# Layer 0's folded sums: four products of 128x32 for two steps, ahead of the weighted values

## The chip, the core and the metric

One core of a Trainium2 chip runs the whole program. The time is device microseconds (us) of one execution; three executions of the kernel before took 980.66, 981.69 and 983.73 us. The core's engines are TensorE (PE in the profile; its weight loads are shown apart as PEld), VectorE (DVE), ScalarE (ACT), GpSimd (POOL) and SyncE (SP). Each engine runs its own instructions in the order of the program and waits on semaphores for the others. SP does nothing here but issue DMAs, which stand in one queue.

## The reference

Two cross attentions follow one another. Both read the same context of 128 keys per batch row; the queries are 2 x 2048 positions of width 512.

```
attn = einsum('bqhd,bkhd->hbqk', qh, kh)          # layer 0: 16 heads of 64
attn = attn * mask
attn = attn - max(attn)                           # one maximum over everything
attn = exp(attn) * mask
attn = attn / (sum(attn, over keys) + 1e-15)
out  = einsum('hbqk,bkhd->bqhd', attn, vh) @ Wo + bo
x    = layernorm(out + residual) * gamma + beta   # and then layer 1 in the same manner
```

What matters here is layer 0's denominator, `sum(attn, over keys)`: for each head and each query one sum over the 128 keys, which lie on the 128 partitions. A sum over partitions is a product with a matrix of ones on TensorE.

## The kernel before, in words

The 4096 queries are eight blocks `t` of 512, the 16 heads four groups `g` of four. A *step* is one pair `(t, g)`. Layer 0 goes through the 32 steps two at a time: `order` (L386) lists them, and the loop at L512 runs 16 iterations `i`, of which iteration `i` makes the scores of steps `2i` and `2i+1` and finishes the two steps of iteration `i-1`. All five engines are scheduled by hand: the order in which the Python code emits instructions is the order on each engine and on SP's queue.

For one iteration after the first the order is:

- `queries_pair` (L336): seven products that make the queries of both steps. Inside it, `exponentials0` (L424) is called for both steps of iteration `i-1`: a maximum on DVE (L430), the exponential on ACT (L434), the mask on POOL (L435). The results are the tiles `sm`, keys on partitions, four heads of 512 queries each.
- `sums_of_folded(i-2)` (L464), if that iteration is in `FOLDED` (L384).
- `scores0` of the first step (L388): four products `st` of 64 rows (L396), two instructions on DVE that apply the mask and take maxima (L409), and two DMAs on SP: a store of the 128x2 maxima, `top` (L418), and a load, `every` (L421), that broadcasts them to all partitions and so waits until the store has landed.
- For iteration `i-1`, if it is in `FOLDED`: `shift` and `fold` of its first step. Then `attend0` of its first step (L477): two sets of four products `psu` (L491) with copies by ACT (L495) and a 512 KB store `u` on SP (L496).
- `shift` of the second step, `scores0` of the second step with its `top` and `every`, `attend0` of the other step of `i-1`, and `fold` of it.

**Folding.** `shift` (L451) has ACT copy one half of the keys of a step's `sm` onto the other 64 partitions, and `fold` (L458) has DVE add the other half. After that 64 partitions hold what has to be summed for one step, and the two steps of an iteration lie in the two halves of one tile `fold` of 128 partitions. `sums_of_folded` then runs, for each of four heads, one product of 64x32 per step, into two PSUM tiles, and `store_sums` (L439) copies each of them to a tile `den` and stores four of its rows on SP (L442).

**Not folded.** `FOLDED` holds eleven iterations: 0, 1, 3, 4, 5, 7, 8, 9, 11, 12 and 13. For the steps of the others, `attend0` makes the sums itself, directly ahead of its `psu`: four products of 128x32 with ones (L484), an ACT copy to a tile `den` and a store. So in the loop's iterations 3, 7, 11 and 15 there are both kinds: the folded sums of `i-2`, and the direct sums of both steps of `i-1` (in the last one, one of these two comes after the loop).

**Tiles that are shared.** The PSUM pool `p_av` (L81) has two buffers, which `sums_of_folded`, `attend0` and two of the seven products take in turn. The pool `a2` has two buffers for each of its tiles, and so there are two of the SBUF tile `den` (L440): the copy that fills one has to wait until the stores that read its previous contents have landed. The tile `fold` has one buffer (pool `w1`, L454).

The line that sets the place of the folded sums is L539 to L545:

```
queries_pair(p, g, order[2 * i - 2 : 2 * i])
if i - 2 in FOLDED:
    sums_of_folded(i - 2)
...
scores0(*steps0[0])
```

After the loop come the last two steps, layer 0's output projection (`pso`, L671) and layer 1. The denominators are read back from DRAM in two halves (L197).

Of the kernel before, what the change touches and what calls it, by code (L numbers as in the profile page):

```python
# [9 lines left out]
F32 = mybir.dt.float32  # L10
# [6 lines left out]
P = 128  # L17
TB = 512
# [6 lines left out]
def two_cross_attentions(  # L25
# [28 lines left out]
    nc = tc.nc  # L54
# [14 lines left out]
    def where(t):  # L69
        return t // SPB, (t % SPB) * TB  # L70
# [5 lines left out]
    const = ctx.enter_context(tc.tile_pool(name="const", bufs=1))  # L76
# [12 lines left out]
    def av_tile(name):  # L89
        return p_av.tile([P, TB], F32, tag="av", name=name)  # L90
# [4 lines left out]
    nc.vector.memset(mhalf, -0.5)  # L95
    ones = const.tile([P, 32], F32, tag="ones", name="ones")
    nc.vector.memset(ones, 1.0)


    idle = mm_tile("idle")  # L100
# [7 lines left out]
    for g in range(NG):  # L108
        for r in range(4):
            rows = slice(32 * r, 32 * (r + 1))  # L110
# [13 lines left out]
    def chunks(w):  # L124
        return w.rearrange("(c p) m -> p c m", p=P)
# [6 lines left out]
    def row(pool, v, name, tag=None):  # L132
# [17 lines left out]
    den_dram = [  # L150
        dram.tile([len(h) * H, TB], F32, tag=f"den_{n}", name=f"den_{n}") for n, h in enumerate(halves)
    ]
# [4 lines left out]
    def den_rows(of, t, g):  # L157
        r0 = (t % (NB // 2)) * H + 4 * g
        return of[t // (NB // 2)][r0 : r0 + 4, :]
# [46 lines left out]
    with tc.tile_pool(name="w1", bufs=1) as w1, tc.tile_pool(name="a2", bufs=2) as a2, tc.tile_pool(  # L206
        name="a3", bufs=3
# [12 lines left out]
        def load_x(t):  # L220

            b, q0 = where(t)
            pool, tag = (big, "big") if t // 2 % 2 else (xs, "xt")
            tiles = []
            for h in range(2):
                xt = pool.tile([P, 2, TB], F32, tag=tag, name=f"xt_{t}_{h}")
                nc.sync.dma_start(xt, xT[b, q0 // TB, h])
                tiles.append(xt)
            xts[t] = tiles

        def load_mask(t):
            b, q0 = where(t)
            m = a4.tile([P, TB], F32, tag="mask", name=f"mask_{t}")
            nc.gpsimd.dma_start(m, maskT[b, :, q0 : q0 + TB])
            return m
# [22 lines left out]
        def keys0(e):  # L258
            ps = mm_tile(f"psk0_{e}")
            for c in range(ND):  # L260
                nc.tensor.matmul(
                    ps[:, : B * K], wk0s[:, e // 2, c, (e % 2) * P : (e % 2 + 1) * P], cTs[:, c, :],
                    start=(c == 0), stop=(c == ND - 1),
                )
            nc.scalar.activation(
                k0[:, e, :], ps[:, : B * K], AF.Identity, bias=bk0s[:, e : e + 1]
            )

        def values0(b, n):
            ps = mm_tile(f"psv0_{b}_{n}")  # L270
            at = slice(n * TB, (n + 1) * TB)
            for c in range(ND):
                nc.tensor.matmul(
                    ps, cTs[:, c, b * K : (b + 1) * K], wv0s[c][:, at],
                    start=(c == 0), stop=(c == ND - 1),
                )
            nc.vector.tensor_tensor(v0[:, b, at], ps, bv0s[n], ALU.add)
# [106 lines left out]
        FOLDED = [n for n in range(NB // 2 * NG - 2) if n % NG != NG - 2]  # L384
        last4 = w1.tile([P, 4], F32, tag="last4", name="last4")
        order = [(2 * p + n, g) for p in range(NB // 2) for g in range(NG) for n in range(2)]  # L386
# [49 lines left out]
                    s, s, masks[t].unsqueeze(1).to_broadcast([P, 2, TB]), ALU.mult  # L436
                )

        def store_sums(t, g, ps, copy=nc.scalar.copy):  # L439
            den = a2.tile([P, TB], F32, tag="den", name=f"dens0_{t}_{g}")  # L440
            copy(den, ps)  # L441
            nc.sync.dma_start(  # L442
                den_rows(den_dram, t, g), den.rearrange("(j n) q -> j n q", n=32)[:, 0, :]
            )

        folded = {}

        def half_keys(n):
            return slice(n * P // 2, (n + 1) * P // 2)

        def shift(i, n):  # L451

            if n == 0:
                folded[i] = w1.tile([P, 4, TB], F32, tag="fold", name=f"fold_{i}")  # L454
            p = pairs0[order[2 * i + n]].rearrange("p n j q -> p (n j) q")
            nc.scalar.copy(folded[i][half_keys(n)], p[half_keys(1 - n)])  # L456

# [5 lines left out]

        def sums_of_folded(i):  # L464
            f = folded.pop(i)
            ps = [av_tile(f"den0_{i}_{n}") for n in range(2)]
            for j in range(4):
                for n in range(2):
                    rows = slice(n * P // 2, (n + 1) * P // 2)
                    nc.tensor.matmul(  # L470
                        ps[n][32 * j : 32 * (j + 1), :], ones[rows, :], f[rows, j, :],
                        start=True, stop=True,
                    )
            for n in range(2):
                store_sums(*order[2 * i + n], ps[n], (nc.vector.tensor_copy, nc.scalar.copy)[n])

        def attend0(t, g):  # L477

            b, _ = where(t)
            p = [probs0[t, 2 * g + j // 2][:, j % 2, :] for j in range(4)]  # L480
            if order.index((t, g)) // 2 not in FOLDED:
                ps = av_tile(f"den0_{t}_{g}")
                for j in range(4):
                    nc.tensor.matmul(ps[32 * j : 32 * (j + 1), :], ones, p[j], start=True, stop=True)  # L484
                store_sums(t, g, ps)
            u = a3.tile([P, 2, TB], F32, tag="u", name=f"u0_{t}_{g}")
            for half in range(2):
                ps = av_tile(f"psu0_{t}_{g}_{half}")
                for j in range(4):
                    d = (4 * g + j) * DK + half * 32  # L490
                    nc.tensor.matmul(  # L491
                        ps[32 * j : 32 * (j + 1), :], v0[:, b, d : d + 32], p[j],
                        start=True, stop=True,
                    )
                nc.scalar.copy(u[:, half, :], ps)  # L495
            nc.sync.dma_start(u_dram[t, g], u.rearrange("p j q -> p (j q)"))  # L496
# [15 lines left out]
        for i in range(len(order) // 2):  # L512
            p, g = i // NG, i % NG
            steps0 = order[2 * i : 2 * i + 2]
            if g == (2 if p == 0 else 1) and p + 1 < NB // 2:
                for t in (2 * p + 2, 2 * p + 3):
                    load_x(t)
                    masks[t] = load_mask(t)
            if p == 0:
                for e in (2 * g, 2 * g + 1):  # L520
                    keys0(e)
            if i == 1:
                for n in range(E // TB):
                    values0(1, n)
            if i == 4:
                w = w1.tile([P, 2 * ND, TB], F32, tag="first", name="wkv1")
                wk1s, wv1s = w[:, :ND, :], w[:, ND:, :]
                nc.sync.dma_start(wk1s, chunks(wk1))
                nc.sync.dma_start(wv1s, chunks(wv1))
            if i == 12:  # L530
                sums0(0, w1, "sums0", 1)
            if i == 13:
                load_wo0()

            if i == 0:
                queries0(0, 0)
                queries0(0, 1)
            else:
                queries_pair(p, g, order[2 * i - 2 : 2 * i])  # L539
                if i - 2 in FOLDED:  # L540
                    sums_of_folded(i - 2)
            if i == len(order) // 2 - 1:
                for n in range(NG):
                    fetch_u(0, n)
            scores0(*steps0[0])  # L545
            if i == 0:
                queries0(1, 0)
                queries0(1, 1)
                weight_sums(1)
            else:  # L550
                if i - 1 in FOLDED:
                    shift(i - 1, 0)
                    fold(i - 1, 0)
                attend0(*order[2 * i - 2])
                if i - 1 in FOLDED:
                    shift(i - 1, 1)
            if i == 0:
                token_sums_1(0)
            elif g == NG - 1 and p + 1 < NB // 2:
                token_sums_1(p + 1)  # L560
            scores0(*steps0[1])
            if i == 0:
                for n in range(E // TB):
                    values0(0, n)
                token_sums_2(0)
                weight_sums(2)
            elif i < len(order) // 2 - 1:
                attend0(*order[2 * i - 1])
                if i - 1 in FOLDED:
                    fold(i - 1, 1)  # L570
            if g == NG - 1 and p + 1 < NB // 2:
                token_sums_2(p + 1)
            if i in (1, 2):
                weight_sums((3, 0)[i - 1])
# [38 lines left out]
        ps = av_tile("whole")  # L613
        nc.tensor.matmul(ps[:, :4], one_row, diag, start=True, stop=True)
        for n in range(2):
            t, g = order[n - 2]
# [532 lines left out]
    t = NB - 1  # L1149
    for i in range(NQ):  # L1150
        project1(t, i, 0)
    for i in range(NQ):
# [5 lines left out]
        else:  # L1158
            ps = open1[t, i]
# [68 lines left out]
```

## Time and profile before

| | |
|---|---|
| time, three executions | 980.66, 981.69, 983.73 us, median 981.69 |
| span of the profiled execution | 977.3 us |
| its own time | not given apart; 4.4 us lie between its span and the median |
| PE busy | 958.0 us, 98% of the span |
| DVE, POOL, ACT busy | 731.8, 483.3, 414.9 us |
| granted TensorE clock, mean | 0.997 |
| folded sums on PE (L470) | 176 instructions in eleven groups, 12.0 us |
| direct sums on PE in the same layer (L484) | 80 instructions in ten groups, 10.7 us |
| DVE copies of sums (L441) | 11 of 692 ns |
| ACT copies of sums (L441) | 21 of 575 ns |
| SP stores of sums (L442) | 32 of 8 KB |

Each f32 product appears as two PE instructions, so sixteen L470 are eight products. A row of the timeline gives the start, how long the merged instructions took, engine, line, output and inputs, and in square brackets how long the engine was idle before and what released it. The ends of matmuls are modelled, so that PE looks busy even where it waits a little; the distance between the starts of two groups is what can be trusted. Of a DMA, SP's row shows the issue alone; when it lands is told by the trace's record of semaphore updates.

### The profile page before, as it was taken

How to read it: one execution, taken by the hardware profiler on the slowest of the kernel's cores; microseconds unless marked ns; L12 is line 12 of the kernel's file. 1: busy time of each engine (PE TensorE's matmuls, PEld its weight loads, DVE VectorE, ACT ScalarE, POOL GpSimd, SP SyncE). 2: the span in 40 equal slices, each digit the busy share in tenths (PEclk: the TensorE clock that was granted, in tenths of full speed). 3: DMA queues.
4: the chain of work that ended last, by engine and by line, in shares of the span. 5: the costliest groups of instructions: out<-in, count | busy, mean ns of one | idle time of the engine just before them, and what ended most of it. 6: DMA issues, size and time to landing. Idle time of an engine off the chain costs nothing.

```text
span 977.3 us, 12755 instructions
## 1 busy us (share of the span) xinstructions
PE 958.0 (98%) x4628; PEld 448.4 (46%) x4628; DVE 731.8 (75%) x1093; ACT 414.9 (42%) x637; POOL 483.3 (49%) x403
## 2 busy tenths in 40 slices
PE   8999999999999999999999999999999999999996
PEld 4444333333333334474544644645545545545442
DVE  2577777878878872249469869879789689698867
ACT  1145345545534644044534434434344444344351
POOL 1044454543453546685453934925835736546153
PEclk9999999999999999999999999999999999999998
DMA  9314265225223436534632542632723724403311
GB/s 337 126 49 141 55 175 155 56 57 182 60 79 86 120 104 201 181 128 157 243 128 87 188 160 87 238 110 89 263 82 119 251 90 155 167 1 151 111 44 43
DMA packets 51325, 128.46 MB, mean 131 GB/s; under 512 B 9440, under 2 KB 13280, under 8 KB 47680
## 3 DMA queue, kind: packets, MB, share of 16 engines
q1 hardware_dynamic: 49536, 125.03, 38.5%
q0 software_dynamic: 1152, 2.10, 0.9%
q8 instruction: 36, 0.59, 0.3%
q10 hardware_dynamic: 576, 0.53, 0.2%
q14 instruction: 25, 0.20, 0.1%
HBM read 101.46 MB, written 26.18 MB: 131 GB/s over the span
## 4 chain that ended last, share of the span: by engine, by line
PE 76%; DVE 4%; POOL 2%; issue 1%; ACT 0%; POOLq 0%; DVEq 0%; ACTq 0%
PE pso L671 22%; PE ps L347 12%; PE pso L1026 10%; PE psq L822 8%; PE psu L491 5%; PE st L396 4%; PE s L948 3%; PE mx L873 3%; PE u L996 3%; PE psq L860 1%; PE tr L727 1%; PE den L470 1%; PE den L484 1%; DVE sums L903 1%; PE psk L591 1%
## 5 line engine op out<-in xcount | busy, mean ns | idle before, releaser
L435 POOL TENSOR_TENSOR sm<-sm,mask 128x1024 f32<-128x1024 f32 x64 | 150.4, 2372 | 202.4 <-ACT sm L434 191.4
L671 PE MATMUL pso<-wo,uT 128*128 128x512 f32 x512 | 229.2, 599 | 0.2 <-POOL uT L182 0.2
L671 PEld LDWEIGHTS pso<-wo,uT 128*128 128x128 f32 x512 | 94.5, 190 | 117.2 <-issue 109.1
L658 POOL TENSOR_TENSOR rstd<-rstd,mhalf 128x1 f32<-128x1 f32 x64 | 35.2, 550 | 213.8 <-DVE shift L662 213.7
L434 ACT ACTIVATE sm<-sm,ncs 128x1024 f32<-128x1024 f32 x64 | 70.0, 1141 | 107.6 <-DVE ncs L431 107.5
L1026 PE MATMUL pso<-wq,ctx 128*128 128x512 f32 x256 | 115.5, 600 | 0.0
L889 ACT ACTIVATE e<-mx,less 128x128 f32<-128x128 f32 x224 | 60.9, 383 | 83.6 <-DVE less L886 83.6
L972 ACT ACTIVATE p<-p 128x2048 f32<-128x2048 f32 x28 | 53.5, 1911 | 97.2 <-DVE p L967 79.5
L409 DVE CUSTOM_DVE_ANT_1 sm<-st,mask 128x1024 f32<-128x1024 f32 x64 | 75.6, 1217 | 20.9 <-DMA mask<-in_maskT_dram 13.5
L967 DVE TENSOR_TENSOR p<-s,p 128x1024 f32<-128x1024 f32 x56 | 65.8, 1217 | 29.2 <-PE s L948 28.6
L347 PE MATMUL ps<-xt,wq 128*128 128x512 f32 x180 | 83.4, 599 | 0.0
L359 DVE TENSOR_TENSOR q<-ps,q 128x512 f32<-128x512 f32 x75 | 51.9, 692 | 39.5 <-PE ps L347 35.3
L182 POOL TENSOR_TENSOR uT<-uT,r 128x1024 f32<-128x1024 f32 x32 | 75.3, 2362 | 3.7 <-issue 1.7
L1026 PEld LDWEIGHTS pso<-wq,ctx 128*128 128x128 f32 x256 | 46.5, 190 | 57.4 <-issue 48.6
L462 DVE TENSOR_TENSOR fold<-fold,sm 64x2048 f32<-64x2048 f32 x22 | 64.5, 2930 | 2.6 <-ACT fold L456 1.9
L903 DVE TENSOR_REDUCE sums<-e 128x16 f32<-128x2048 f32 x28 | 63.8, 2278 | 1.1 <-ACT e L897 1.1
L396 PE MATMUL st<-q,k 64*128 64x512 f32 x256 | 63.6, 615 | 0.0
L491 PE MATMUL psu<-sm,v 128*32 128x512 f32 x512 | 62.1, 598 | 0.8 <-ACT dens L441 0.7
L347 PE MATMUL ps<-t,s 128*128 128x512 f32 x120 | 56.4, 592 | 0.0
L347 PEld LDWEIGHTS ps<-xt,wq 128*128 128x128 f32 x180 | 33.2, 190 | 46.5 <-issue 46.4
L686 ACT ACTIVATE z<-z,shift,rstd 128x512 f32<-128x512 f32 x32 | 26.0, 814 | 66.9 <-POOL shift L663 66.9
L688 POOL TENSOR_TENSOR y<-z,g 128x512 f32<-128x512 f32 x32 | 40.6, 1269 | 23.1 <-ACT z L686 23.1
(154 smaller groups left out, 1511.0 us busy)
## 6 DMA issues: line engine op xcount, KB each, us to landing
p<-rows SPq DMA_DIRECT2D x28, 1024.0 KB
u<-u SPq DMA_DIRECT2D x32, 512.0 KB
uT<-u SPq DMA_DIRECT2D x32, 512.0 KB
xt<-in_xT_dram SPq DMA_DIRECT2D x16, 512.0 KB
z<-in_x_dram SPq DMA_DIRECT2D x32, 256.0 KB
r<-r SPq DMA_DIRECT2D x32, 256.0 KB
out_dram<-y SPq DMA_DIRECT2D x32, 256.0 KB
r<-rows SPq DMA_DIRECT2D x28, 256.0 KB
```

The costliest lines, as they stand in the source:

```text
L182: nc.gpsimd.tensor_tensor(u, u, r.unsqueeze(1).to_broadcast([P, 2, TB]), ALU.mult)
L347: nc.tensor.matmul(ps, w[:, c, :], x[c] if isinstance(x, tuple) else x[:, c, :], start=(c == 0), stop=(c == 1),)
L396: nc.tensor.matmul(st[n][:, j, :], k0[rows, 2 * g + n, b * K : (b + 1) * K], q[rows, :], start=True, stop=True,)
L409: nc.vector.tensor_tensor_reduce(out=sm, in0=st[n], in1=masks[t].unsqueeze(1).to_broadcast([P, 2, TB]), scale=1.0, scalar=-3.4028234e38, o ...
L434: nc.scalar.activation(s, s, AF.Exp, bias=ncs[:, i + n : i + n + 1])
L435: nc.gpsimd.tensor_tensor(s, s, masks[t].unsqueeze(1).to_broadcast([P, 2, TB]), ALU.mult)
L491: nc.tensor.matmul(ps[32 * j : 32 * (j + 1), :], v0[:, b, d : d + 32], p[j], start=True, stop=True,)
L671: nc.tensor.matmul(ps, uTs[t, n // 2][:, n % 2, i * P : (i + 1) * P], wo0s[n // 2][:, n % 2, :], start=(n == 0), stop=(n == NE - 1),)
L822: nc.tensor.matmul(ps[:, m, :], w[:, c, m * P : (m + 1) * P], y[:, c, :], start=(c == 0), stop=(c == 1),)
L903: nc.vector.tensor_reduce(to.rearrange("p r i o -> p r (i o)"), open_x.pop((t, g)), AX.X, ALU.add)
L967: nc.vector.tensor_tensor(p1[:, at], ps[n], p1[:, at], ALU.subtract)
L1026: nc.tensor.matmul(ps, ctxs[t][g][:, i * P : (i + 1) * P], wo1s[:, g, :], start=(g == 0), stop=(g == NG - 1),)
```

## The change

The two steps' sums come from one product per head. A new constant `both` of 128x32 holds ones for the first 64 partitions in its columns 0 to 15, and ones for the last 64 in columns 16 to 31. One product of `both` with a head's 128 partitions of `fold` thus gives the first step's sums in 16 rows and the second step's in the 16 after them. Eight products of 64x32 into two PSUM tiles become four of 128x32 into one. One ACT copy takes the place of a DVE copy and an ACT copy; the two stores of four rows remain, and read one `den` tile.

`sums_of_folded(i-2)` moves from ahead of the first step's `scores0` to behind it, directly ahead of `shift`, `fold` and `attend0`. `fold` gets a second buffer, and to make room in SBUF the DMA scratch is set to 2048 bytes per partition.

```diff
+    both = const.tile([P, 2, 16], F32, tag="both", name="both")
+    nc.vector.memset(both, 0.0)
+    for n in range(2):
+        nc.vector.memset(both[n * P // 2 : (n + 1) * P // 2, n, :], 1.0)
+    both = both.rearrange("p n m -> p (n m)")
...
-        def store_sums(t, g, ps, copy=nc.scalar.copy):
-            den = a2.tile([P, TB], F32, tag="den", name=f"dens0_{t}_{g}")
+        def store_sums(steps, ps, copy):
+            den = a2.tile([P, TB], F32, tag="den", name=f"dens0_{steps[0][0]}_{steps[0][1]}")
             copy(den, ps)
-            nc.sync.dma_start(
-                den_rows(den_dram, t, g), den.rearrange("(j n) q -> j n q", n=32)[:, 0, :]
-            )
+            rows = den.rearrange("(j n) q -> j n q", n=32)
+            for n, (t, g) in enumerate(steps):
+                nc.sync.dma_start(den_rows(den_dram, t, g), rows[:, 16 * n, :])
...
-                folded[i] = w1.tile([P, 4, TB], F32, tag="fold", name=f"fold_{i}")
+                folded[i] = w1.tile([P, 4, TB], F32, tag="fold", bufs=2, name=f"fold_{i}")
...
             f = folded.pop(i)
-            ps = [av_tile(f"den0_{i}_{n}") for n in range(2)]
+            ps = av_tile(f"den0_{i}")
             for j in range(4):
-                for n in range(2):
-                    rows = slice(n * P // 2, (n + 1) * P // 2)
-                    nc.tensor.matmul(
-                        ps[n][32 * j : 32 * (j + 1), :], ones[rows, :], f[rows, j, :],
-                        start=True, stop=True,
-                    )
-            for n in range(2):
-                store_sums(*order[2 * i + n], ps[n], (nc.vector.tensor_copy, nc.scalar.copy)[n])
+                nc.tensor.matmul(ps[32 * j : 32 * (j + 1), :], both, f[:, j, :], start=True, stop=True)
+            store_sums(order[2 * i : 2 * i + 2], ps, nc.scalar.copy)
...
-                store_sums(t, g, ps)
+                store_sums([(t, g)], ps, nc.scalar.copy)
...
                 queries_pair(p, g, order[2 * i - 2 : 2 * i])
-                if i - 2 in FOLDED:
-                    sums_of_folded(i - 2)
...
             scores0(*steps0[0])
...
             else:
+                if i - 2 in FOLDED:
+                    sums_of_folded(i - 2)
                 if i - 1 in FOLDED:
                     shift(i - 1, 0)
...
-    nc = bacc.Bacc("TRN2", target_bir_lowering=False, num_devices=1)
+    nc = bacc.Bacc("TRN2", target_bir_lowering=False, num_devices=1, dynamic_dma_scratch_size=2048)
```

## The prediction

> **What bounds the kernel now.** I read the page's busy times first, then PE's timeline around the sums, then the queues beside it.
>
> ```profile
> PE 958.0 (98%) x4628; PEld 448.4 (46%) x4628; DVE 731.8 (75%) x1093; ACT 414.9 (42%) x637; POOL 483.3 (49%) x403
> ```
>
> PE is the bound. Since the ends of matmuls are modelled, I go by distances between starts. This is PE in iteration 11, which has folded sums (L470) and direct sums (L484):
>
> ```profile
> 272.20 1.88 PE L347 MATMUL ps<-xt,s 128*128 128x512 f32 x4
> 274.01 1.09 PE L470 MATMUL den<-fold,ones 64*32 64x512 f32 x16
> 275.03 1.99 PE L396 MATMUL st<-q,k 64*128 64x512 f32 x8
> 276.95 1.06 PE L484 MATMUL den<-sm,ones 128*32 128x512 f32 x8
> 277.83 1.96 PE L491 MATMUL psu<-sm,v 128*32 128x512 f32 x16
> 279.72 1.99 PE L396 MATMUL st<-q,k 64*128 64x512 f32 x8
> 281.64 1.06 PE L484 MATMUL den<-sm,ones 128*32 128x512 f32 x8
> 282.52 2.00 PE L491 MATMUL psu<-sm,v 128*32 128x512 f32 x16
> 284.45 1.98 PE L347 MATMUL ps<-xt,wq 128*128 128x512 f32 x4
> ```
>
> Folded sums hold PE for 275.03-274.01 = 1.02 us; direct sums, which have the form that the change gives to the folded ones, for 277.83-276.95 = 0.88. The group behind is spaced the same whether or not sums stand ahead of it: L347 to st takes 1.81 in iteration 12, as L347 to L470 does here. Over layer 0's loop these distances hardly vary, so PE runs without pauses. The exceptions are st to psu at 148.66 (2.72 for 1.92, a wait for ACT's copy of sums) and at 317.44 (2.06).
>
> Next the two queues that the sums use, in the same iteration, SP and ACT:
>
> ```profile
> 275.91 1.07 SPq L442 DMA_DIRECT2D den<-dens  x2
> 278.61 0.32 SPq L418 DMA_DIRECT2D top<-top  x1
> 281.45 0.33 SPq L421 DMA_DIRECT2D every<-top  x1
> 281.88 0.50 SPq L442 DMA_DIRECT2D den<-dens  x1
> 282.43 0.44 SPq L496 DMA_DIRECT2D u<-u  x1
> ```
>
> ```profile
> 275.81 0.56 ACT L441 COPY dens<-den 128x512 f32<-128x512 f32 x1
> 278.08 0.59 ACT L441 COPY dens<-den 128x512 f32<-128x512 f32 x1 [1.71 <-PE den L484]
> ...
> 282.81 0.59 ACT L441 COPY dens<-den 128x512 f32<-128x512 f32 x1 [2.37 <-PE den L484]
> ```
>
> The folded stores go out before `top`. SP then waits from 278.93 to 281.45 for `top` to land before it may issue `every`. ACT's two later copies wait for PE alone. The record of semaphore updates tells the landings: the two folded stores, issued 275.91 and 276.50, landed at 277.57 and 278.16, 1.66 us after issue. The direct store issued at 281.88, right behind the broadcast `every`, landed at 285.63, after 3.75; its siblings in iterations 3 and 7 took 3.73 and 3.42. The windows show why it is so late:
>
> ```profile
> 281.40:283.40 2.00, 2.00 (x18) 0.42 (x16) 1.97 (x5) 0.59 (x1) 0.00 (x0) 1.00 0.00 0
> 283.40:285.70 2.30, 2.30 (x15) 0.83 (x12) 2.30 (x6) 1.18 (x2) 0.00 (x0) 1.00 0.92 176
> ```
>
> (last two columns: DMA share, GB/s). The queue moves nothing for 2 us after the broadcast's issue, then everything at once.
>
> **PE's share of the change.** I count from s, where L470 starts before (274.01 here). Before: sums 1.02, st 1.92, psu 1.86, which makes st of the second step start at 4.79 in an undisturbed iteration without direct sums. After: st 1.92, sums 0.88, psu 1.89 (behind direct sums it takes 1.89 to 1.93, as it waits for the copy), so 4.69. That is 0.10 for each of eleven groups. Three of them had small pauses that go too: 4.84 (iteration 9), 4.93 (13) and 5.59 (5). In the last ACT's exponentials end at s+3.13, so the one copy ends at 3.8 and the second psu set starts some 0.2 late instead of 0.8. Sum: 8 x 0.10 + 0.15 + 0.24 + 0.70 = 1.9 us gained. Bounds: 0.8 (each psu 0.1 later than taken) to 2.8 (psu at 1.86, sums at their busy 0.86, no pause left).
>
> **What lies beside PE.** The DVE copy removed (11 x 0.69 us) stood between two DVE waits for PE, so it is worth nothing by itself; DVE's L409 simply comes 1.02 earlier with st. ACT keeps one copy, but at s+3.05 instead of 1.80, since it waits for sums that now end there (L484 to its copy: 1.13). `shift` behind it so ends at 5.55 instead of 4.29, and DVE's `fold` starts at 5.55 instead of 4.49. That costs almost nothing, as DVE did not get on before POOL was done: fold takes 2.29 alone and 3.30 where POOL's mask runs to 5.65, so it ended at 7.79 and will end at 7.9. ACT's copies of `u` end at 6.1 and 6.7 (4.77 and 5.51 before), while the next psu needs the first buffer at 6.6: cover of 0.5 us. If it is gone, each of seven iterations pays up to 0.5. Three memsets on DVE lie in the first 20 us, of which DVE is busy for 3.9; soon after it waits 13.5 for a mask. The second `fold` buffer takes away a wait that would otherwise stand between `shift` and the sums. [...]
>
> **The stores, and who waits for them.** Each folded group's two stores move past `top` and `every` on SP. `top` goes out 1.02 earlier, at s+3.58 (before 4.60); it lands 2.76 later, so `every` is issued at 6.42. The folded stores follow at 6.85 and 7.44, where they were at 1.90 and 2.49. Behind them stand the direct store and `u`, at 8.6 instead of 8.42: nothing, as the second `top` comes at 10.4.
>
> The contents of these stores are not needed for long. Their tile is. `den` has two buffers. Before, a folded group took both, and the direct sums of iterations 3, 7 and 11 took them again after the stores had landed at s+3.56 and 4.15. Now a folded group takes one, the first direct sums the other, and the second direct sums take the folded group's again. Their copy is ready to start at s+8.66 (8.80 before, less 0.14). But the folded stores, issued behind the broadcast, have not landed. The first one stands exactly where the direct store stood (0.43 behind `every`), so I take the mean of its three rows, 3.63: s+10.48. The second shares the queue and is issued 0.59 later; I put it 0.3 behind, at 10.8.
>
> So ACT's copy starts at 10.85 and ends at 11.44. That copy frees the PSUM buffer which the second set of the second psu needs. PE wants it at 7.53+0.88+0.86+0.05 = 9.3 and gets it at about 11.5: 2.2 us in which PE, on the path that sets the end, stands still. Nothing absorbs it, as PE is packed behind it too. Iteration 15 is spared: it has no `top` and `every`, and its second direct sums come after the loop. Iterations without direct sums take one `den` each and never catch up with the stores. Cost: 3 x 2.2 = 6.6 us.
>
> Bounds of one such wait: with the quiet landing of 1.66 the second store is in at 9.10 and the wait is 0.5; with the slowest row (3.90, the store behind the second `every` of iteration 11) it is 7.44+3.90 = 11.34, and the wait 2.7; with the fastest row behind a broadcast (3.42) and both stores landing together, 10.27 and 1.7. I take the rows behind a broadcast, because the new place is theirs.
>
> [...]
>
> **Sum.** -1.9 + 6.6 = +4.7 us: the profiled execution's 977.3 becomes 982.0, and with the 4.4 us between the span and the median 986.4. With the bounds: -2.8 + 3 x 1.7 = +2.3 to -0.8 + 3 x 2.7 = +7.3, so 984.0 to 989.0 for this case alone.
>
> **Rivals.** What a measurement of this kernel can tell from no change is about 0.3%, 2.9 us.
>
> 1. *No wait for `den`: PE's gain stays.* For it: stores landed within 1.66 us in a quiet queue. Against: the three rows behind `every`. Decided by the landing of the second folded store: before s+8.66 there is no wait, and the time is 981.7-1.9 = 979.8; with 0.5 each it is 981.3. On either count not slower, chance 0.17.
> 2. *ACT's later copies stall PE in the other iterations too.* For it: cover of only 0.5 us at the second psu. Against: POOL and ACT run there in fixed steps, and release by a copy takes below 0.1. Price 7 x 0.5 = 3.5 on top: 989.9. Chance 0.10.
> 3. *The gain is at its bound and no wait comes*: -2.8, 978.9, about the edge of what counts as faster; more would need a pause of PE that the distances don't show. Chance 0.05.
>
> **How the numbers follow.** The forecast has 0.68. Slower by over 0.3% (above 984.6): 0.62 of it (it reaches below 984.6 only where both bounds meet) and rival 2, 0.72. Within 0.3%: its lower tail 0.06 and nearly all of rival 1, 0.22. Faster: 0.06, from rival 3 and a little of rival 1. The range has to reach into rival 1's partial wait and most of rival 2: 981.0 to 989.6.
>
> **What the profile after would show.** Eleven groups of eight instructions of folded sums between st and the next group, 0.88 long, and L347 followed by st at 1.81. SP issuing the folded stores 0.4 behind `every`. In three places, and only there, an ACT copy of sums whose wait ends with a store's landing, followed by psu waiting for ACT for some 2 us. PE's span of layer 0 longer by 4.7, everything after it the same. Wrong would be: ACT's copies all released by PE; psu waiting in iterations without direct sums; or `fold` ending well after s+8 and holding back DVE.

## The result and the profile after

The changed kernel takes 989.31 us (median; 987.83 to 989.59) against 982.71 for the kernel before on the same chip: a ratio of 1.0065, 95% interval 1.0048 to 1.0082. It is slower, by 6.6 us where 4.7 had been forecast, and lies inside the stated range of 981.0 to 989.6, 0.3 us below its upper end. Of the 2.9 us between the measured time and the forecast's 986.4, 1.9 is the larger loss; the other 1.0 is that the kernel before took 982.71 here and not 981.69.

PE in iteration 11 after the change (timeline: start, length, engine, line, what; in brackets the idle time before and what ended it). L473 are the folded sums now, L483 the direct ones, L490 the weighted values:

```profile
278.62 1.88 PE L352 MATMUL ps<-xt,s 128*128 128x512 f32 x4
280.43 1.99 PE L401 MATMUL st<-q,k 64*128 64x512 f32 x8
282.34 1.07 PE L473 MATMUL den<-fold,both 128*32 128x512 f32 x8
283.23 1.04 PE L483 MATMUL den<-sm,ones 128*32 128x512 f32 x8
284.12 1.97 PE L490 MATMUL psu<-sm,v 128*32 128x512 f32 x16
286.01 1.99 PE L401 MATMUL st<-q,k 64*128 64x512 f32 x8
287.93 1.06 PE L483 MATMUL den<-sm,ones 128*32 128x512 f32 x8
288.81 1.04 PE L490 MATMUL psu<-sm,v 128*32 128x512 f32 x8
291.86 1.06 PE L490 MATMUL psu<-sm,v 128*32 128x512 f32 x8 [2.00 <-ACT dens L446]
292.85 1.98 PE L352 MATMUL ps<-xt,wq 128*128 128x512 f32 x4
```

The sums hold PE for 283.23-282.34 = 0.89 us, and L352 is followed by st after 1.81, both as forecast. The last psu is now in two pieces with PE idle between them. SP's queue and ACT in the same iteration show why:

```profile
284.01 0.32 SPq L423 DMA_DIRECT2D top<-top  x1
286.82 0.32 SPq L426 DMA_DIRECT2D every<-top  x1
287.23 1.60 SPq L449 DMA_DIRECT2D den<-dens  x3
288.88 0.43 SPq L495 DMA_DIRECT2D u<-u  x1
```

```profile
283.48 0.59 ACT L446 COPY dens<-den 128x512 f32<-128x512 f32 x1 [1.16 <-PE den L473]
284.38 0.59 ACT L446 COPY dens<-den 128x512 f32<-128x512 f32 x1 [0.31 <-PE den L483]
...
291.22 0.59 ACT L446 COPY dens<-den 128x512 f32<-128x512 f32 x1 [4.48 <-DMA den<-dens]
```

The folded stores (the first two of three L449) stand 0.41 behind the broadcast `every`, 3.16 after the copy that makes them ready has ended (283.48+0.59 to 287.23). By the record of semaphore updates they were issued at 287.23 and 287.78 and landed at 290.88 and 291.06, 3.65 and 3.28 us later. ACT's third copy, at 291.22, begins when the second has landed. The waits of PE and ACT over the whole of layer 0's loop (who waited for whom: us in total, times, the longest) say that this happens three times and that little else stops PE there:

```profile
PE psu L490 <- ACT dens L446: 6.5, 3, 2.5
```

```profile
ACT dens L446 <- DMA den<-dens: 13.9, 3, 4.9
```

One thing was not forecast. After the wait in iteration 7, the next products run at half speed (the windows' last three columns are the granted clock, the DMA share and GB/s):

```profile
199.49 1.06 PE L483 MATMUL den<-sm,ones 128*32 128x512 f32 x8
200.38 1.04 PE L490 MATMUL psu<-sm,v 128*32 128x512 f32 x8
203.87 1.21 PE L490 MATMUL psu<-sm,v 128*32 128x512 f32 x8 [2.46 <-ACT dens L446]
205.01 3.49 PE L352 MATMUL ps<-xt,wq 128*128 128x512 f32 x4
208.34 1.88 PE L352 MATMUL ps<-t,s 128*128 128x512 f32 x4
```

```profile
203.80:206.00 2.20, 2.13 (x9) 0.66 (x10) 1.64 (x4) 1.09 (x3) 0.00 (x0) 0.70 0.07 17
206.00:208.30 2.30, 2.30 (x4) 1.01 (x3) 0.00 (x0) 0.00 (x0) 0.00 (x0) 0.55 0.00 0
208.30:212.00 3.70, 3.70 (x10) 1.71 (x9) 0.72 (x2) 2.76 (x3) 1.66 (x1) 1.00 0.47 179
```

Four L352 take 3.33 to the next group, where they take 1.72 to 1.82 elsewhere. The trace's clock record has the clock at a half from 204.67 to 208.08, 3.41 us, and nowhere else but at the very end.

**Where the time went**, by the two profiled executions (spans 977.3 and 987.1 us, 9.8 apart):

- The first st starts 0.44 later, before any of the change.
- Layer 0's loop is 7.5 longer, measured from the first st to the start of the output projection. The three waits, read as psu to the next L352 less the 1.93 that this takes there before, are 2.1, 2.7 and 2.1. Half clock costs 1.5 in the queries behind the second of them. Five small waits of 0.1 to 0.4 at psu in iterations 6, 9 and 10 come to 1.2. Against these stands a gain of some 2.2.
- Behind the loop another 1.9 is lost, half of it in the projection, where PE waits 1.0 for POOL's `uT`. This does not look like a loss by the change: the stretch from the start of the projection to the end takes 588.3 in the profile of the kernel before, which is the shortest of all the runs here, 590.2 in this one, and between 589.0 and 591.7 in the others, 589.8 of them in the kernel before with nothing but the second `fold` buffer and the smaller scratch.

The medians are only 6.6 apart. The kernel before had been profiled in an execution quicker than its median: what lies around a span is 989.15-987.10 = 2.05 us in the run after, and 977.3+2.05 = 979.4.

### The profile page after: what moved, and what is told of

Read it like the earlier page. It is cut to its first block, busy times and chain, and to the rows that moved or that the text cites. A ratio compares the mean times of both kernels' runs of the same rounds, so it can differ in the third digit from the quotient of the medians.

```text
span 987.1 us, 12536 instructions
## 1 busy us (share of the span) xinstructions
PE 962.2 (97%) x4540; PEld 451.6 (46%) x4540; DVE 725.5 (74%) x1085; ACT 414.5 (42%) x637; POOL 483.3 (49%) x403
## 4 chain that ended last, share of the span: by engine, by line
PE 85%; DVE 5%; DMA 5%; POOL 2%; issue 1%; ACT 1%; SPq 0%; POOLq 0%; ACTq 0%; DVEq 0%
PE pso L670 21%; PE ps L352 19%; PE pso L1025 9%; PE psq L821 7%; PE st L401 5%; PE psu L490 5%; PE mx L872 3%; PE s L947 3%; PE u L995 3%; DMA r<-rows 2%; PE psk L266 2%; PE psq L859 1%; PE psq L333 1%; PE psv L278 1%; DMA r<-r 1%
## 5 line engine op out<-in xcount | busy, mean ns | idle before, releaser
L352 PE MATMUL ps<-xt,wq 128*128 128x512 f32 x180 | 84.9, 608 | 0.0
L467 DVE TENSOR_TENSOR fold<-fold,sm 64x2048 f32<-64x2048 f32 x22 | 61.5, 2795 | 14.8 <-ACT fold L461 14.5
L490 PE MATMUL psu<-sm,v 128*32 128x512 f32 x512 | 64.0, 600 | 6.6 <-ACT dens L446 6.5
L352 PE MATMUL ps<-t,s 128*128 128x512 f32 x120 | 56.4, 592 | 0.0
L352 PEld LDWEIGHTS ps<-xt,wq 128*128 128x128 f32 x180 | 33.7, 193 | 47.2 <-issue 46.4
```

Source lines behind the costliest of these rows:

```text
L352: nc.tensor.matmul(ps, w[:, c, :], x[c] if isinstance(x, tuple) else x[:, c, :], start=(c == 0), stop=(c == 1),)
L490: nc.tensor.matmul(ps[32 * j : 32 * (j + 1), :], v0[:, b, d : d + 32], p[j], start=True, stop=True,)
```

## The experiments

The theories. *Theory 1*, that of the forecast: the second direct sums' copy waits for the buffer of the folded sums' `den`, whose stores stand behind the broadcast in SP's queue. *Theory 2*: the sums behind the scores make ACT's `shift` and copies of `u` late, and psu waits for those. *Theory 3*: the second `fold` buffer and the smaller scratch. Each ratio is against the kernel before, run beside the experiment: 980.82 us for the first four, 982.16 for the last four.

### A third buffer for `den`

```diff
-            den = a2.tile([P, TB], F32, tag="den", name=...)
+            den = a2.tile([P, TB], F32, tag="den", bufs=3, name=...)
```

> The changed kernel with a third buffer for the tile den, nothing else. If the loss is the second direct sums' copy waiting for the folded stores (theory 1), the three waits of ACT for a landing and the 6.5 us of PE behind them go, and with them the stretch at half clock: 1.0 to 2.5 us faster than the kernel before, a ratio of 0.9975 to 0.999. If it is ACT's later shift and u copies (theory 2), it stays at about 1.0065. If it is the second fold buffer or the smaller scratch (theory 3), also 1.0065.

Measured: 978.71 us against 980.82, a ratio of 0.9977 (0.9968 to 0.9985). All three waits of PE are gone. PE in layer 0's loop waits for nothing that the profile puts down, the granted clock is 1.00 there (in iteration 7 the four L352 behind psu take 1.82, from 199.78 to 201.60), and ACT's copy in iteration 7 is released by PE:

```profile
198.15 0.58 ACT L446 COPY dens<-den 128x512 f32<-128x512 f32 x1 [2.37 <-PE den L483]
```

In iteration 11 it is the same; in iteration 3 the profile puts the same 2.37 down to a landing, and PE loses nothing by it.

One buffer of 2 KB per partition turns 6.6 us lost into 2.1 gained. Theory 2 and theory 3 are out as causes of the loss, since the place, the second `fold` buffer and the scratch are the same here as in the change.

### The stores between the two DMAs of the maxima

```diff
-            scores0(*steps0[0])
+            late = i - 2 in FOLDED and i < len(order) // 2 - 1
+            scores0(*steps0[0], whole=not late)      # top alone
...
                 if i - 2 in FOLDED:
                     sums_of_folded(i - 2)
+                if late:
+                    load_tops(*steps0[0])            # every
```

> The changed kernel, in which the broadcast load of the first step's maxima is issued behind the folded stores instead of ahead of them: on SP the order is top, folded stores, every. The stores are ready at about 3.7 us from the start of st, while SP waits for top until 6.3 anyway, so every should go out no later. Theory 1: stores land by about 6.5, no wait for den, ratio 0.9975 to 0.999 as with the third buffer. Theory 2 and 3: 1.0065. If the stores delay every, DVE's maxima would wait and the ratio would lie above that of the third buffer.

Measured: 978.72 against 980.82, 0.9981 (0.9972 to 0.9990), with two `den` buffers as in the change. SP in iteration 7:

```profile
192.21 0.32 SPq L423 DMA_DIRECT2D top<-top  x1
192.62 1.03 SPq L453 DMA_DIRECT2D den<-dens  x2
195.55 0.32 SPq L430 DMA_DIRECT2D every<-top  x1
```

and ACT's copy for the second direct sums:

```profile
197.31 0.58 ACT L450 COPY dens<-den 128x512 f32<-128x512 f32 x1 [2.37 <-PE den L487]
```

The folded stores use the time in which SP waits for `top` anyway, and landed 2.51 and 2.13 us after issue, the second at 195.30, before ACT's copy was ready at 197.31. `every` comes 3.34 behind `top`; in the changed kernel it was 3.25 in this iteration. So it is not the sharing of `den` that costs, nor the place on PE, but the place in SP's queue together with the sharing. Two things come with that place, a later issue (3.16 us after the copy in the change) and a slower landing (3.2 to 3.7 us instead of 2.1 to 2.5); no run sets them apart.

### The place undone, the new products alone

```diff
                 queries_pair(p, g, order[2 * i - 2 : 2 * i])
+                if i - 2 in FOLDED:
+                    sums_of_folded(i - 2)
...
-                if i - 2 in FOLDED:
-                    sums_of_folded(i - 2)
                 if i - 1 in FOLDED:
```

> The changed kernel with the folded sums back in their old place, ahead of the first step's scores: the one product per head and the one copy are tried alone. The stores go out ahead of top again, so theory 1 expects no wait for den; theory 2 expects no late shift either. Both: 0.998 to 1.000. PE's distance from the start of the sums to st tells what the form is worth by itself: 0.88 us if it is the form, 1.02 as before if it is the place.

Measured: 980.66 against 980.82, 0.9999 (0.9990 to 1.0008).

```profile
187.03 1.88 PE L352 MATMUL ps<-xt,s 128*128 128x512 f32 x4
188.84 1.06 PE L473 MATMUL den<-fold,both 128*32 128x512 f32 x8
189.83 1.99 PE L401 MATMUL st<-q,k 64*128 64x512 f32 x8
```

In the old place the new products hold PE for 0.99 us, where the old ones held it for 1.02 and the same new ones take 0.88 ahead of psu. Of the 0.14 us per group, 0.03 is the form, and 0.11 goes with the place; why, no run shows. The forecast had put all of it down together. Half as many products are by themselves worth eleven times 0.03, which is less than this comparison can see.

### The room alone

```diff
-                folded[i] = w1.tile([P, 4, TB], F32, tag="fold", name=f"fold_{i}")
+                folded[i] = w1.tile([P, 4, TB], F32, tag="fold", bufs=2, name=f"fold_{i}")
...
+    nc = bacc.Bacc(..., dynamic_dma_scratch_size=2048)
```

> The kernel before with the second fold buffer and the smaller DMA scratch alone. Theories 1 and 2: no difference, 0.998 to 1.002. Theory 3: about 1.0065.

Measured: 981.23 against 980.82, 1.0001 (0.9988 to 1.0013): no difference, and the forecast's sum has no term for the room.

### More ahead of the stores

```diff
                 if i - 2 in FOLDED:
+                    if i in (3, 7, 11):
+                        extra = a2.tile([P, 2 * P], F32, tag="extra", name=f"extra_{i}")
+                        flat = top_dram[steps0[0]].rearrange("p n -> (p n)").unsqueeze(0)
+                        nc.sync.dma_start(extra, flat.to_broadcast([P, 2 * P]))
                     sums_of_folded(i - 2)
```

> The changed kernel with one more broadcast load of 128 KB (into a tile that nobody reads) on SP, ahead of the folded stores in iterations 3, 7 and 11. If the wait for den is set by what stands ahead of the stores in SP's queue, each of the three waits grows from about 2.3 us to 4 or 4.5, some 6 us in sum. The profile of the changed kernel showed one stretch of 3.4 us at half TensorE clock behind its longest wait (2.46), and none behind the two shorter ones (2.0); with waits above 4 there should be such a stretch behind all three, 1.7 us each, of which one was there before: 3 more. Ratio about 1.015. If the loss hangs on something else than what is queued ahead, 1.007.

Measured: 997.83 against 982.16, 1.0155 (1.0138 to 1.0172). The folded stores of iteration 3 landed 5.23 and 4.87 us after issue and those of iteration 11 4.80 and 4.43; those of iteration 7 landed after 3.99 and 3.61, but SP had issued them about 1 us later than the others. PE waited

```profile
PE psu L490 <- ACT dens L446: 11.5, 3, 3.9
```

Read as psu to the next L352 less 1.93, the waits are 4.5, 4.8 and 3.9, where 4 or 4.5 had been expected. Half clock followed every one of the three, as expected, but for 3.41, 6.83 and 3.41 us: the second stretch was twice as long. So the waits, 2.1, 2.7 and 2.1 in the changed kernel, were longer with more queued ahead of the stores.

### The move alone

```diff
                 queries_pair(p, g, order[2 * i - 2 : 2 * i])
-                if i - 2 in FOLDED:
-                    sums_of_folded(i - 2)
...
             else:
+                if i - 2 in FOLDED:
+                    sums_of_folded(i - 2)
                 if i - 1 in FOLDED:
                     shift(i - 1, 0)
```

The products, PSUM tiles and copies are those of the kernel before; second `fold` buffer and scratch as in the change.

> The kernel before with the move alone: eight products of 64x32, two PSUM tiles, two den tiles and two copies (DVE and ACT) as before, but behind the first step's scores; second fold buffer and smaller scratch as in the change. A folded group now takes both den buffers, and so the first direct sums' copy in iterations 3, 7 and 11 has to wait for a store behind the broadcast: ready about 4.9 us after st's start, let go at about 10.6, a wait of PE of 5 to 6 us in each, and half clock behind it. Theory 1: 3 x 5.5 + 3 x 1.7, less nothing for PE's form: 15 to 24 us slower, ratio 1.015 to 1.024. If the single den tile of the folded sums were what hurts, this would be no slower than before.

Measured: 1016.42 against 982.16, 1.0345 (1.0330 to 1.0361), 34 us, where 15 to 24 had been expected. Iteration 7:

```profile
202.01 1.99 PE L396 MATMUL st<-q,k 64*128 64x512 f32 x8
203.93 1.09 PE L470 MATMUL den<-fold,ones 64*32 64x512 f32 x16
205.92 1.06 PE L484 MATMUL den<-sm,ones 128*32 128x512 f32 x8 [0.91 <-ACT dens L441]
206.78 1.07 PE L491 MATMUL psu<-sm,v 128*32 128x512 f32 x8
213.33 1.94 PE L491 MATMUL psu<-sm,v 128*32 128x512 f32 x8 [5.48 <-ACT dens L441]
215.19 3.79 PE L396 MATMUL st<-q,k 64*128 64x512 f32 x8
```

The wait of 5.5 us and half clock behind it were expected; that each stretch of half clock would last 6.83 us and not 3.41 was not. Together they cost 6.4 to 6.6 from psu to the next group and 1.7 to 1.8 at the half-speed st, in each of three iterations: some 25 in sum. What was missed is the distance of 1.99 from the sums to the next group, instead of 1.02. Two PSUM tiles of sums directly ahead of psu fill both buffers of the pool, and PE has to wait for a copy; that is about 0.95 in each of eleven groups, 10 us. So it is the one PSUM tile for two steps that spares the new place this wait.

### The folded stores on ACT's queue

```diff
             for n, (t, g) in enumerate(steps):
-                nc.sync.dma_start(den_rows(den_dram, t, g), rows[:, 16 * n, :])
+                (nc.scalar if len(steps) == 2 else nc.sync).dma_start(den_rows(den_dram, t, g), rows[:, 16 * n, :])
```

> The changed kernel with the folded stores issued from ACT's queue instead of SP's, in the same place; the direct stores stay on SP. They no longer stand behind the broadcast, so theory 1 expects landings some 2 us after the copy and no wait for den: the gain of the third buffer, less what two issues on ACT cost there (0.5 us each ahead of shift, in eleven iterations): u's copies would then be later than the second psu needs by some 0.5, ratio 0.998 to 1.002. If landings are late by the two tiles' stores alone, wherever they are issued, 1.006.

Measured: 987.16 against 982.16, 1.0048 (1.0033 to 1.0063): slower, outside what was expected. The waits for landings at the three places are indeed gone, and the granted clock is 1.00 in the loop. The stores go out as soon as their copy is done and are in when the second direct sums need the tile, although they took 2.7 to 4.1 us from issue to landing, where some 2 had been expected. Instead PE now waits in every folded group:

```profile
PE psu L490 <- ACT u L494: 4.6, 7, 1.1
PE psu L490 <- ACT dens L446: 2.8, 4, 0.9
```

```profile
238.43 0.56 ACT L446 COPY dens<-den 128x512 f32<-128x512 f32 x1
239.02 1.01 ACTq L449 DMA_DIRECT2D den<-dens  x2
240.07 1.90 ACT L461 COPY fold<-sm 64x2048 f32<-64x2048 f32 x1 [1.08 <-POOL sm L440]
241.87 1.06 ACT L494 COPY u<-psu 128x512 f32<-128x512 f32 x2
```

Two issues take ACT 1.0 us, what stands behind them is later, and psu waits 0.57 (st to psu is 2.56 to 2.58 for 1.92 in six of the seven iterations without direct sums, and 3.14 in the first). This is theory 2's mechanism, made on purpose, and measures its cover: 1.0 us of delay costs 0.6, so some 0.4 was free, where the forecast had 0.5.

### The changed kernel once more

The kernel of the change, with nothing edited.

> The changed kernel once more, unchanged, beside the others: 1.005 to 1.008. Of interest is how often half clock follows its waits: behind a wait above 2.4 us if a length decides, at any of the three places if it is a matter of when the wait falls.

Measured: 989.71 against 982.16, 1.0076 (1.0060 to 1.0091). PE's three waits are 1.96, 2.18 and 2.17:

```profile
116.57 1.87 PE L490 MATMUL psu<-sm,v 128*32 128x512 f32 x8 [1.96 <-ACT dens L446]
204.43 1.06 PE L490 MATMUL psu<-sm,v 128*32 128x512 f32 x8 [2.18 <-ACT dens L446]
292.27 1.06 PE L490 MATMUL psu<-sm,v 128*32 128x512 f32 x8 [2.17 <-ACT dens L446]
```

Half clock follows the first (116.70 to 120.12) and the second (205.45 to 208.86) but not the third. So length alone does not decide: 1.96 us was followed by it and 2.17 was not. What does, no run shows.

## Why the prediction was right

- **Direction and cause: right.** The three waits are where the forecast put them, in iterations 3, 7 and 11 at the second psu, and for the reason given. With s the start of st in iteration 11 (280.43), the first folded store was issued at s+6.80 (forecast 6.85) and landed at 10.45 (10.48); the second landed at 10.63 (10.8); ACT's copy started at 10.79 (10.85), and PE went on at 11.43 (11.5). A third buffer takes the loss away, and more in the queue adds to it.
- **Size of the loss: 2.2 for each wait was about right, and half clock behind a wait was left out.** The waits came to 7.0 instead of 6.6; in iteration 7 `every` went out 3.25 us behind `top`, in iteration 11 2.81. Half clock adds one stretch (about 1.7 us) in one profiled execution of the changed kernel and two in the other; a forecast of PE standing still for 2 us should have asked whether its clock stays up. This is the main term missing from the sum; the small waits of 1.2 are the other.
- **PE's gain: right in size, and in part by luck.** 1.9 was forecast; 2.1 was measured by the medians with the waits removed in two ways. In the profile with the third buffer an iteration with a folded group is 0.11 shorter, and 0.16 where there are direct sums too, 1.4 in eleven groups where 0.10 each had been forecast; most of that goes with the place and not with the number of products. The rest of the forecast, 0.8, was small pauses of one profiled execution that would go. They change from one execution to the next: with the room alone one of 0.9 is in iteration 9, in the profile before one of 0.8 in iteration 5.
- **DVE, ACT, POOL: right with a correction.** Without DVE's copy, in the old place, the time was the same (0.9999), so it was worth nothing that shows. With the third buffer PE waits for nothing in the loop, so ACT's later `shift` and what DVE does behind it were in time. The cover of 0.5 us ahead of the second psu was 0.4, by the run with ACT's queue. The five small waits of the changed kernel begin elsewhere: in iterations 6, 9 and 10 DVE waits 1.45, 1.34 and 0.95 us for a broadcast `every`, and ACT's exponentials start 0.75 to 1.26 behind st, where they start 0.29 ahead of it in iteration 7. The pauses of the kernel before, in iterations 5, 9 and 13, begin with such a wait as well. In the loop DVE waits for `every` three times in the kernel before, seven times in both profiles of the changed one and never with the third buffer; why, the runs do not tell.
- **The first rival** (no wait for `den`) is what the kernel does with a third buffer; the gain that it stood for, 1.9, was right for that (2.1). **The second** (ACT's copies stall PE in the other iterations) holds only in part: 1.2 us instead of 3.5, and begun by a late `every`. **The third** (the gain at its bound and no wait) is out, because the waits came.
- **What lies around the span: wrong.** 4.4 us had been put there from the median; it is 2.05, and the profiled execution was 2.3 faster than the median. It cancels in the difference, on which the forecast rests. That everything after layer 0 would be the same is borne out only as far as its spread allows, 588.3 to 591.7.

The two versions with the waits removed take 0.9977 and 0.9981 of the time of the kernel before, where the changed kernel takes 1.0065 of it; they are thus the fastest of all that was run, by 0.2% against the kernel before and, by the quotient of these ratios, by some 0.9% against the changed one.

## What to carry to other kernels

When work is moved behind a step, list what that step puts into the DMA queue, and follow each store of the moved work to the buffer that it frees: nobody read these sums back for some 100 us or more (the stores of iteration 7 went out at 199 us, the load that reads them at 297), but the next user of their tile stood ready some 1.4 us after they were issued. Small stores belong into a gap in which the queue's engine waits anyway, here between a store and the load that needs it (with the two stores in it, SP still waited from 193.65 to 195.55 in iteration 7). And count the buffers that are taken at the new place: with two `den` tiles for a folded group the same move cost 34 us, since the first direct sums already had to wait; with one it cost 6.6, since only the second had to; with a third buffer none had to.

## What the runs showed of the hardware

**Half clock behind a wait of PE.** In the two profiled executions of the changed kernel PE was idle for 2.04, 2.46 and 2.00 us at the three places in the one, and for 1.96, 2.18 and 2.17 in the other. The granted clock was a half for 3.41 us behind the waits of 2.46, 1.96 and 2.18, and 1.00 behind the other three. In the three cases the distance from the second half of psu to the second L352 group behind it was 4.47, 4.47 and 4.50 us, where it is 2.81 at full clock: such a wait cost 1.7 more or nothing. Behind the waits of 3.70 to 3.93 us in the run with the extra broadcast half clock followed each time, for 3.41, 6.83 and 3.41 us; behind the long ones of the move alone (5.48 in iteration 7) it lasted 6.83 each time. Behind the one wait of PE in the loop of the kernel before, 0.73 us in iteration 5, the clock was 1.00. No run set out to vary the length of a wait or when it falls, so what decides whether half clock follows, and for how long, is not shown.

**A small store behind a broadcast load on the same queue.** The folded stores of iterations 3, 7 and 11 landed 3.2 to 3.7 us after their issue in the changed kernel (3.1 to 4.0 over all ten groups behind a broadcast; 1.66 in iteration 15, which has none). In the kernel before they took 1.64 to 1.77 in eight of the eleven groups and 2.4 to 4.5 in the other three. In the run that puts them between `top` and `every` they took 2.51 and 2.13 in iteration 7. The queue is not all of it: on ACT's queue, with no broadcast ahead of them and SP's store of `top` issued 0.1 us before, the same stores took 2.7 to 4.1.
